# A macaron block with a state-space layer on one Trainium2 core: turning the down projection's result by 32x32 blocks and a round trip through HBM

## The chip, the cores and the metric

The kernel runs on one core of a Trainium2 chip. The metric is device time in microseconds (us) of the whole program, which is one launch. The engines of the core are called PE (TensorE, matrix products), DVE (VectorE), ACT (ScalarE), POOL (GpSimd) and SP (SyncE, which in this kernel issues nearly all DMAs).

## The reference

The input `u` is two sequences of 1024 rows with 1024 columns, 2048 rows in all, in fp32. Three residual steps follow each other:

```python
x = x + 0.5 * ffn(layernorm(x))      # gate, up and down: 4-bit weights, INTER = 2752
x = x + s4(layernorm(x))             # a causal filter along each row, by a Toeplitz product
x = x + 0.5 * ffn(layernorm(x))      # the same weights again

def ffn(x):
    h = silu(x @ Wg) * (x @ Wu)      # 1024 -> 2752
    return h @ Wd                    # 2752 -> 1024
```

The weights are stored as packed 4-bit numbers with a scale and a zero point for each group of 128 input rows and each output column. The result is fp32.

## The kernel before, in words

The 2048 rows are four blocks `b` of TB = 512 rows. A feed-forward pass over one block is a job; the list `JOBS` holds eight, `(0,1) (1,1) (0,3) (1,3) (2,1) (3,1) (2,3) (3,3)`, the second number being 1 for the first feed-forward of the block and 3 for the second. A block's filter (`convolve`) and layernorms are done in the shadow of another block's job.

**A job** has two stages. `gate_up(j, b, hooks)` runs 64 steps. A step is one wave of two or three 128-column groups with one of eight 128-row groups of the weights. In a wave of three there are six accumulators in PSUM and twelve matrix products in a step: each accumulator takes a product with the high part (`xTh`, fp32) and one with the low part (`xTl`, fp16) of the turned input (L753). After a step each accumulator is multiplied in place by the ratio of two groups' scales, by `scaled`: on ACT (L723) or on DVE (L725). Then the next step adds to it. `down(j, b, hooks)` runs 44 steps, `a` = 0, 1 for the two halves of 512 output columns and `f` = 0 to 21 for the rows of Wd. A step has four accumulators, `c` = 0 to 3, each with two products (`hl` and `hh`, L825) and one scaling; `c` = 0 and 2 go to ACT, `c` = 1 and 3 to DVE. At the last `f` the scaled result is written to SBUF: `yT[a, c]`, a tile of 128 output columns by 512 rows of the block. So the result lies turned, columns on partitions, while `x` has rows on partitions.

**Bringing the result back.** `back(b, a, t)` handles 128 rows and 512 columns. PE turns four 128x128 pieces of `yT` into a PSUM bank (L847), and DVE adds the bank to `x[b][t]` (L849). A job has eight calls, 2 halves by 4 values of `t`.

**The order around it.** Work of other stages is put into dictionaries of hooks, `up` and `dn`, by step number. A hook is called when its step is written, ahead of the step's products. `at(hooks, s, f)` adds one. The instructions of an engine then run in the order in which the tile scheduler puts them; `in_order_of_writing(f, engines)` pins the instructions of `f` to their written place on the engines named. Back of half 0 is at `dn` steps 26, 30, 34, 38 (32, 35, 38, 41 in job 0), after `load_x` has brought the block's `x` again at step 21; back of half 1 is at `up` steps 0 to 3 of the next job, and after the last job's end for the last one. For blocks whose first feed-forward is over, the next job's `up` also holds `moments` and `deviations` (layernorm statistics, at steps 4 and 5), and from step 8 (42 in job 1) `norm`, `swap` and `conv`, four steps for each `t`. `normalize` (L256) and `turn_by_dma` prepare the next job's input, the latter with POOL operations and transposing DMAs on SP at `dn` steps.

**The weights' supply.** `next_weights` issues on SP the load of the bytes for four steps ahead (`b<-wq`, `bd<-wdq`) and writes the cast to fp32 on POOL for three steps ahead (L701).

**Buffers.** `ypool` has four tiles of 128x512 fp32; `convolve` takes two of them for each `t`. `xpool` has ten tiles of 128x1024, `hpool` 44 tiles of 128x512.

Of the kernel before, what the change touches and what calls it, by code (L numbers as in the profile page):

```python
# [24 lines left out]
P = 128  # L25
# [3 lines left out]
TB = 512  # L29
# [11 lines left out]
EIGHT = 8.0  # L41
LIFT = 2.0**20
NST = 64
EPS = 1e-5
LOG2E = 1.4426950408889634
LN2_HI = 0.693359375
# [9 lines left out]
def macaron_s4_kernel(  # L56
# [43 lines left out]
    qpool = ctx.enter_context(tc.tile_pool(name="q", bufs=4))  # L100
    gpool = ctx.enter_context(tc.tile_pool(name="g", bufs=3))
    hfpool = ctx.enter_context(tc.tile_pool(name="hf", bufs=3))
    ypool = ctx.enter_context(tc.tile_pool(name="y", bufs=4))
    ppool = ctx.enter_context(tc.tile_pool(name="ps", bufs=1, space=PSUM))
    dpool = ctx.enter_context(tc.tile_pool(name="dram", bufs=1, space=DRAM))

# [310 lines left out]
    def scales_down():  # L417
        ps = bank("ps_d")
        for i in range(2):
            row = t2(f"drow_{i}")  # L420
            nc.sync.dma_start(row[:GD], down_s[:, bass.ts(i, 512)])
            for k in range(4):
                nc.tensor.transpose(
                    ps[:, bass.ts(4 * i + k, GD)], row[:GD, bass.ts(k, P)], ident[:GD, :GD]
                )
        n = NC * GD
        flat = s_dn.rearrange("p c g -> p (c g)")
        nc.vector.tensor_copy(flat, ps[:, :n])
        inv = t2("inv_d")[:, :n]
        inverse(inv, flat, "d")  # L430
        inv = inv.rearrange("p (c g) -> p c g", c=NC)
        nc.vector.tensor_tensor(
            ratd[:, :, : GD - 1], s_dn[:, :, : GD - 1], inv[:, :, 1:], ALU.mult
        )
        nc.vector.tensor_scalar(
            ratd[:, :, GD - 1 :], s_dn[:, :, GD - 1 :], 0.5 / EIGHT, None, ALU.mult
        )
# [44 lines left out]
    def units(w):  # L482
# [2 lines left out]
        return got + [2 * WIDE] * (w == len(WAVES) - 1)  # L485

    width_of = lambda w: len(units(w)) * P
    w_q = [
        dpool.tile([HID, width_of(w)], I8, tag=f"wq{w}", name=f"wq{w}") for w in range(len(WAVES))
    ]  # L490
# [142 lines left out]
    def dequantize_down(a, rt, j):  # L633
        src = packed[a, rt][j % 2][:, j // 2, :]
        n = src.shape[0]
        q = qpool.tile([P, 512], I8, tag="q", name=f"qd_{a}_{rt}_{j}")[:n]
        nc.gpsimd.tensor_copy(q, src)
        rows = wd_q[a][8 * P * rt : 8 * P * rt + 8 * n]
        nc.sync.dma_start(rows.rearrange("(r j) n -> j r n", j=8)[j], q)
        if j == 7:  # L640
            packed.pop((a, rt))
# [75 lines left out]


    h = {}

    def scaled(on_act, dst, src, sc):
        if on_act:
            nc.scalar.activation(dst, src, AF.Copy, scale=sc)  # L723
        else:
            nc.vector.tensor_tensor(dst, src, sc.to_broadcast([P, TB]), ALU.mult)  # L725

    def gate_up(j, b, hooks):
        hi, lo = pieces[b]
        ps = {}
        for s, (wi, g) in enumerate(STEPS):  # L730
            w = next_weights()
            for hook in hooks.get(s, ()):
                hook()
            fs = WAVES[wi]
            n = len(fs)
            order = [(2 * f + i, i * n + u) for u, f in enumerate(fs) for i in range(2)]
            if wi == len(WAVES) - 1:
                order.append((2 * WIDE, 2 * n))


            early = len(order) // 2
            turns = [(k, pos, k == 1) for k in range(2) for pos in range(early)]
            turns += [(k, pos, k == 0) for k in (1, 0) for pos in range(early, len(order))]
            for k, pos, done in turns:
                unit, col = order[pos]
                if g == 0 and unit not in ps:
                    ps[unit] = acc(f"pg_{j}_{unit}")
                p = ps[unit]
                weights = w[:, bass.ts(col, P)]
                if k == 0:  # L750

                    weights = weights.bitcast(BF16).rearrange("p (n k) -> p k n", k=2)[:, 1, :]
                nc.tensor.matmul(  # L753
                    p,
                    weights,
                    (lo, hi)[k][:, g, :],
                    start=(g == 0 and not done),
                    stop=(g == GK - 1 and done),
                    skip_group_check=True,
                )  # L760
                if not done:
                    continue
                if g < GK - 1:
                    on_act = unit % 2 == 0
                    if pos == 1:
                        on_act = (j == 0 and g % 4 == 0) or (j == 1 and s < 32 and g % 2 == 0)
                    if unit == 2 * WIDE:
                        on_act = g % 2 == 0
                    scaled(on_act, p, p, rat[:, unit, g : g + 1])
                elif unit == 2 * WIDE:  # L770
                    gated_half(j, ps[unit])
                    give_back(ps.pop(unit))
                elif unit % 2:
                    gated(j, unit // 2, ps[unit - 1], ps[unit])
                    give_back(ps.pop(unit - 1), ps.pop(unit))
        pieces.pop(b)
# [37 lines left out]
    def down(j, b, hooks):  # L814

        steps = [(a, f) for a in range(NH) for f in range(NF)]
        for d, (a, f) in enumerate(steps):
# [3 lines left out]
            if f == 0:  # L821
                ps = [acc(f"po_{j}_{a}_{c}") for c in range(4)]
            for c in range(4):
                for k, part in enumerate(reversed(h[f])):
                    nc.tensor.matmul(  # L825
                        ps[c],
                        w[:, bass.ts(c, P)],
                        part,
                        start=(f == 0 and k == 0),
                        stop=(f == NF - 1),  # L830
                        skip_group_check=True,
                    )
                on_act = c % 2 == 0 or (j == 0 and c == 1 and f % 2 == 0)
                if f < GD - 1:
                    scaled(on_act, ps[c], ps[c], ratd[:, 4 * a + c, f : f + 1])
                elif f == NF - 1:
                    y = ypool.tile([P, TB], F32, tag="y", name=f"y_{j}_{a}_{c}")
                    scaled(on_act, y, ps[c], ratd[:, 4 * a + c, GD - 1 :])
                    yT[a, c] = y
                    give_back(ps[c])  # L840
        h.clear()

    def back(b, a, t):

        ps = bank(f"pb_{b}_{a}_{t}")
        for c in range(4):
            nc.tensor.transpose(ps[:, bass.ts(c, P)], yT[a, c][:, bass.ts(t, P)], ident)  # L847
        part = x[b][t][:, bass.ts(a, 512)]
        nc.vector.tensor_tensor(part, part, ps, ALU.add)  # L849

    near = const.tile([P, 4, P], F32, tag="near", name="near")
    after = const.tile([P, 4, P], F32, tag="after", name="after")
# [279 lines left out]
    def convolve(b, t, s, name):  # L1137
# [1 line left out]

        sums = ypool.tile([P, TB], F32, tag="y", name=f"sums_{name}")
        sums = sums.rearrange("p (c t) -> p c t", c=4)
        quad = ypool.tile([P, TB], F32, tag="y", name=f"quad_{name}")
        quad = quad[:, : 2 * P].rearrange("p (c t) -> p c t", c=2)
        nc.gpsimd.tensor_tensor(sums[:, 0:3], s[:, 0:6:2, :], s[:, 1:6:2, :], ALU.add)
        nc.gpsimd.tensor_tensor(quad, s[:, 0:2, :], s[:, 2:4, :], ALU.add)
        nc.gpsimd.tensor_tensor(sums[:, 3], sums[:, 0], sums[:, 1], ALU.add)
# [266 lines left out]

    x_dram = [dpool.tile([P, HID], F32, tag=f"xs{t}", name=f"xs{t}") for t in range(TOK // P)]
    saved = lambda b: x_dram[b * NT : (b + 1) * NT]
    JOBS = [(0, 1), (1, 1), (0, 3), (1, 3), (2, 1), (3, 1), (2, 3), (3, 3)]

    def fast():  # L1420
        def store_half(t, a, queue):
# [4 lines left out]
        for j, (b, k) in enumerate(JOBS):  # L1426
# [4 lines left out]
            def at(hooks, s, f):  # L1431
                hooks.setdefault(s, []).append(f)

            if prev:
                pb, pk = prev
                for t in range(NT):
                    at(up, t, lambda t=t: back(pb, 1, t))
                if pk == 1:
                    late = 34 if j == 1 else 0
                    at(up, 4, lambda: moments(pb, 2))  # L1440
                    at(up, 5, lambda: deviations(pb, 2))
                    s4x, s4n = {}, {}

                    def norm(t):
# [23 lines left out]
                    at(up, late + 28, save)  # L1468
                else:

                    def store():
                        for t, dst in enumerate(rows_of(out, pb)):
                            nc.sync.dma_start(dst, x[pb][t])
                        x.pop(pb)

                    at(up, 4, store)
            if j == 0:
                rows = {3: srow_next}
                for first_use, s, k0, k1 in ((5, 0, 3, 9), (14, 6, 9, 15), (30, 11, 15, WIDE)):
# [18 lines left out]
            if after:  # L1498
# [22 lines left out]
                for t in range(NT):  # L1521
                    for half in range(2):
                        d, where = ((22 + 4 * t + 2 * half, dn), (3 * t + half, dn))[min(j, 1)]
                        if j > 1:
                            d, where = 31 + 2 * t + half, up
                        piece = lambda t=t, half=half: normalize(ab, t, half)
                        piece = lambda piece=piece: in_order_of_writing(piece, ET.DVE)
                        at(where, d, piece)
# [10 lines left out]
            for d in (1, 2) if j else ():  # L1539
                piece = lambda j=j: next(half_split[j], None)  # L1540
                at(dn, d, lambda piece=piece: in_order_of_writing(piece, ET.Pool))
            o, gap = (27, 3) if j == 0 else (21, 4)
            at(dn, o, lambda: load_x(b, rows_of(u, b) if k == 1 else saved(b)))
            for t in range(NT):
                at(dn, o + 5 + gap * t, lambda t=t: back(b, 0, t))
                if not after:
                    first_half = lambda t=t: store_half(t, 0, nc.sync)
                    at(dn, o + 6 + gap * t, first_half)
            gate_up(j, b, up)
            down(j, b, dn)  # L1550
        for t in range(NT):
            back(b, 1, t)
            store_half(t, 1, (nc.sync, nc.scalar)[t % 2])

    STARTING = ET.Activation, ET.DVE, ET.SP
# [200 lines left out]
```

## Time and profile before

| | |
|---|---|
| time, median of 3 runs | 2096.85 us (2094.32 to 2098.55) |
| span of the profiled execution | 2095.8 us; its own time outside the profile is not given |
| mean granted TensorE clock | 0.998 |
| PE busy | 2054.6 us, 98% of the span |
| DVE busy | 1671.5 us, 80% |
| ACT busy | 1398.9 us, 67% |
| POOL busy | 1291.6 us, 62% |
| DMA moved | 151.03 MB, 24.7% of 16 engines' span on the main queue |

Busy time is the time in which an engine has at least one instruction at work. PE's matrix products overlap each other in the records, so a product of 435 ns costs less than that on the path: twelve in a row take about 2.7 us. The chain of waits is the better view for PE, since it splits the path without overlap.

### The profile page before, as it was taken

What the parts mean: (1) busy time and instruction counts of PE and PEld (TensorE: products, weight loads), DVE (VectorE), ACT (ScalarE), POOL (GpSimd) and SP (SyncE); (2) the same over time, 40 slices, a digit from 0 to 9 for tenths busy, and PEclk for the clock granted to TensorE, in tenths of its full rate; (3) what the DMA queues carried; (4) which work ended last, traced back from release to release, by engine and by line L of the source; (5) the groups of instructions that cost most, each with busy time, mean ns of one, the idle gap of its engine ahead of it and who ended that gap; (6) DMA issues with size and microseconds to landing.
All of it is one profiled execution on the core that took longest, in us unless ns stands there. A gap on an engine that the chain in (4) does not pass through costs nothing.

```text
span 2095.8 us, 30242 instructions
## 1 busy us (share of the span) xinstructions
PE 2054.6 (98%) x9556; PEld 1410.6 (67%) x9556; DVE 1671.5 (80%) x2749; ACT 1398.9 (67%) x2185; POOL 1291.6 (62%) x1688
## 2 busy tenths in 40 slices
PE   6999999999999999999999999999999999999998
PEld 4555775677776578655876568675686766866576
DVE  8888887778888877797778878878788787777776
ACT  6777777746655776667667776547765467667775
POOL 5867758657754577555955568455684546845542
PEclk9999999999999999999999999999999999999999
DMA  4324321113411126211441124111151111531111
GB/s 144 119 85 146 111 66 54 36 56 74 110 39 55 32 53 170 72 31 36 122 137 37 31 51 126 44 51 32 46 130 37 51 39 35 133 128 36 33 35 60
DMA packets 239719, 151.03 MB, mean 72 GB/s; under 512 B 98747, under 2 KB 226596, under 8 KB 239550
## 3 DMA queue, kind: packets, MB, share of 16 engines
q1 hardware_dynamic: 238246, 146.60, 24.7%
q8 instruction: 78, 1.28, 0.3%
q10 hardware_dynamic: 1016, 1.82, 0.2%
q14 instruction: 91, 0.75, 0.1%
q0 software_dynamic: 288, 0.59, 0.1%
HBM read 104.45 MB, written 25.50 MB: 62 GB/s over the span
## 4 chain that ended last, share of the span: by engine, by line
PE 92%; DVE 4%; DMA 1%; ACT 1%; issue 1%; POOL 0%; SPq 0%; ACTq 0%; DVEq 0%; POOLq 0%
PE pg L753 56%; PE po L825 29%; PE pc L1151 3%; PE pb L847 1%; PE pb L1151 1%; DVE pg L725 1%; PE st L230 1%; DMA b<-wq 1%; ACT g L780 0%; DVE po L725 0%; DVE x L256 0%; DMA x<-in_L_attn_u_dram 0%; POOL q L608 0%; DVE hf L783 0%; PE pt L230 0%
## 5 line engine op out<-in xcount | busy, mean ns | idle before, releaser
L723 ACT ACTIVATE pg<-pg,rat 128x512 f32<-128x512 f32 x1240 | 787.5, 661 | 418.1 <-PE pg L753 415.9
L725 DVE TENSOR_TENSOR pg<-pg,rat 128x512 f32<-128x512 f32 x1168 | 776.6, 693 | 159.3 <-PE pg L753 153.4
L753 PE MATMUL pg<-xTh,w_up 128*128 128x512 f32 x2752 | 840.5, 435 | 1.1 <-DVE pg L725 0.7
L753 PE MATMUL pg<-xTl,w_up 128*128 128x512 f16 x2752 | 716.7, 382 | 11.6 <-DVE pg L725 5.6
L701 POOL CAST w_up<-b 128x768 fp32r<-128x768 int8 (+2 forms) x490 | 378.0, 777 | 504.6 <-PE pg L753 405.7
L753 PEld LDWEIGHTS pg<-xTh,w_up 128*128 128x128 f32 x2752 | 518.3, 189 | 175.9 <-DVE pg L725 12.2
L723 ACT ACTIVATE po<-po,ratd 128x512 f32<-128x512 f32 x660 | 431.8, 661 | 164.7 <-PE po L825 164.1
L825 PE MATMUL po<-hl,w_down 128*128 128x512 f32 x1344 | 530.5, 397 | 3.7 <-DVE po L725 3.6
L825 PE MATMUL po<-hh,w_down 128*128 128x512 f32 x1344 | 521.2, 390 | 0.0
L725 DVE TENSOR_TENSOR po<-po,ratd 128x512 f32<-128x512 f32 x620 | 430.4, 698 | 113.3 <-PE po L825 109.1
L753 PEld LDWEIGHTS <-w_up 128*128 128x128 bf16 x2752 | 228.4, 99 | 330.3 <-issue 151.0
L701 POOL CAST w_down<-bd 128x512 fp32r<-128x512 int8 x352 | 218.4, 624 | 158.5 <-PE po L825 90.4
L825 PEld LDWEIGHTS po<-hl,w_down 128*128 128x128 f32 x1344 | 251.2, 188 | 73.3 <-DVE po L725 12.2
L825 PEld LDWEIGHTS po<-hh,w_down 128*128 128x128 f32 x1344 | 252.6, 188 | 49.0
L787 POOL TENSOR_TENSOR hl<-hf,hh 128x512 fp32r<-128x512 f32 x168 | 217.9, 1297 | 8.0
L783 DVE SCALAR_TENSOR_TENSOR hf<-pg,rat,g 128x512 f32<-128x512 f32 x168 | 123.2, 749 | 49.3 <-ACT g L780 40.4
L780 ACT ACTIVATE g<-pg,rat 128x512 f32<-128x512 f32 x168 | 111.0, 687 | 48.5 <-PE pg L753 32.8
L785 POOL CAST hh<-hf 128x512 fp32r<-128x512 f32 x168 | 106.1, 632 | 55.0 <-PE pg L753 31.0
L282 POOL TENSOR_TENSOR lo<-x,hi 128x512 f16<-128x512 f32 x48 | 62.2, 1296 | 0.0
L187 DVE BATCH_NORM_STATS2 stats<-x 128x6 f32<-128x512 f32 x88 | 60.0, 682 | 0.5
L280 POOL TENSOR_TENSOR mid<-hi,top 128x512 bf16<-128x512 f32 x48 | 56.4, 1174 | 0.0
L296 POOL TENSOR_TENSOR xTh<-turned 128x512 fp32r<-128x512 bf16 x48 | 55.9, 1165 | 0.0
(216 smaller groups left out, 1104.2 us busy)
## 6 DMA issues: line engine op xcount, KB each, us to landing
b<-wq SPq DMA_DIRECT2D x319, 96.0 KB
bd<-wdq SPq DMA_DIRECT2D x336, 64.0 KB
x<-in_L_attn_u_dram SPq DMA_DIRECT2D x30, 512.0 KB
b<-wq SPq DMA_DIRECT2D x128, 64.0 KB
xs<-x SPq DMA_DIRECT2D x16, 512.0 KB
x<-xs SPq DMA_DIRECT2D x16, 512.0 KB
out_dram<-x SPq DMA_DIRECT2D x12, 512.0 KB
b<-wq SPq DMA_DIRECT2D x64, 80.0 KB
```

The source lines that it names most:

```text
L187: nc.vector.bn_stats(stats[:, t, i, :], x[b][t][:, bass.ts(i, 512)])
L282: nc.gpsimd.tensor_tensor(lo[:, own], n[:, own], hi[:, own].bitcast(F32), ALU.subtract)
L701: nc.gpsimd.tensor_copy(t, b)
L723: nc.scalar.activation(dst, src, AF.Copy, scale=sc)
L725: nc.vector.tensor_tensor(dst, src, sc.to_broadcast([P, TB]), ALU.mult)
L753: nc.tensor.matmul(p, weights, (lo, hi)[k][:, g, :], start=(g == 0 and not done), stop=(g == GK - 1 and done), skip_group_check=True,)
L780: nc.scalar.activation(g, pg, AF.Silu, scale=rat[:, 2 * f, GK - 1 :])
L783: nc.vector.scalar_tensor_tensor(hf, pu, last, g, ALU.mult, ALU.mult)
L785: nc.gpsimd.tensor_copy(hi, hf)
L787: nc.gpsimd.tensor_tensor(lo, hf, hi.bitcast(F32), ALU.subtract)
L825: nc.tensor.matmul(ps[c], w[:, bass.ts(c, P)], part, start=(f == 0 and k == 0), stop=(f == NF - 1), skip_group_check=True,)
L1151: nc.tensor.matmul(dst, lhsT, rhs, start=start, stop=stop, skip_group_check=True)
```

## The change

Half results are no longer turned by PE, but for the last half of the last job.

- `yT[a]` is one tile of 128 x 2048 fp32 (`ypool` with one buffer). The weights' columns of Wd are stored in a permuted order (`by_block`, `by_chunk`), by `dequantize_down` on POOL and by `scales_down` on DVE, so that the four 32-row bands of the partitions and the four `c` hold columns that come out in sequence.
- The last scaling writes each `c` in runs of 32 (`block_of`). `turn_block` then turns eight 32x32 blocks in place with one DVE instruction on 128x256 elements; there are eight for each half.
- `rows_out` stores a band of 32 partitions to `y_dram[a]`, 256 KB in runs of 512 bytes, four DMAs on SP for each half. `rows_in` loads 128 rows by 512 columns, 256 KB, four for each half, into tiles of `hpool`.
- `back` is now a DVE addition on 128x256 with both inputs in SBUF, eight for each half. The last half of the last job keeps the products (`back_by_products`).
- `rows_home` puts these at steps: half 0 at `dn` 22 to 25.5 (turn), 27 and 28 (out), 31 and 32 (in), 34.5 to 41.5 (add); half 1 at `up` 0 to 3.5, 5 and 6, 8 and 9, 10 to 13.5 of the next job. Job 0's half 0 and job 1's half 1 have spacings of their own. Hooks may now stand at half steps: `gate_up` and `down` call those of `s + 0.5` in the middle of a step.
- Moved with it: in jobs 2, 5 and 6 the first `moments` of the filter goes from step 4 to pinned pieces at steps 14 to 19, and what follows it 14 steps later; in job 1 it goes to steps 30 to 38. In these jobs `normalize` for a second feed-forward goes from `up` step 31 to 45. The stores of finished blocks go from one hook at step 4 to four at steps 13 to 16. In jobs 2, 5 and 6 at steps 10 to 19, every second step's accumulator at place 1 is scaled on ACT.
- `convolve` takes its two temporaries from the one `y` tile.

The diff, cut to its core:

```diff
-    ypool = ctx.enter_context(tc.tile_pool(name="y", bufs=4))
+    ypool = ctx.enter_context(tc.tile_pool(name="y", bufs=1))
...
+            nc.vector.tensor_copy(by_chunk(turn[:GD]), by_block(row[:GD]))
...
+    by_block = lambda a: a.rearrange("p (a c i) -> p a c i", a=NQ, i=Q)
+    by_chunk = lambda a: a.rearrange("p (c a i) -> p a c i", a=NQ, i=Q)
...
-        nc.gpsimd.tensor_copy(q, src)
+        nc.gpsimd.tensor_copy(by_chunk(q), by_block(src))
...
+                        on_act = on_act or (j in (2, 5, 6) and 10 <= s < 20 and g % 2 == 0)
...
-                    y = ypool.tile([P, TB], F32, tag="y", name=f"y_{j}_{a}_{c}")
-                    scaled(on_act, y, ps[c], ratd[:, 4 * a + c, GD - 1 :])
-                    yT[a, c] = y
+                    if c == 0:
+                        yT[a] = ypool.tile([P, 4 * TB], F32, tag="y", name=f"y_{j}_{a}")
+                    if by_products(j, a):
+                        y = yT[a][:, bass.ts(c, TB)]
+                        scaled(on_act, y, ps[c], ratd[:, 4 * a + c, GD - 1 :])
+                    else:
+                        y, p = block_of(yT[a], c), ps[c].rearrange("p (t i) -> p t i", i=Q)
+                        scaled(on_act, y, p, ratd[:, 4 * a + c, GD - 1 :])
...
+    def block_of(y, c):
+        return y.rearrange("p (t c i) -> p t c i", c=4, i=Q)[:, :, c]
+    def turn_block(a, i):
+        c, half = divmod(i, 2)
+        part = block_of(yT[a], c)[:, bass.ts(half, TB // Q // 2)]
+        nc.vector.transpose(part, part)
+    def rows_out(a, q):
+        src = yT[a][bass.ts(q, Q)].rearrange("p (t n) -> p t n", n=P)
+        dst = y_dram[a].rearrange("(t i) (a n) -> a i t n", i=Q, n=P)[q]
+        nc.sync.dma_start(dst, src)
+    def rows_in(b, a, t):
+        rows_back[a, t] = r = t2(f"yr_{b}_{a}_{t}")
+        nc.sync.dma_start(r, y_dram[a][bass.ts(t, P)])
-    def back(b, a, t):
-        ps = bank(f"pb_{b}_{a}_{t}")
-        for c in range(4):
-            nc.tensor.transpose(ps[:, bass.ts(c, P)], yT[a, c][:, bass.ts(t, P)], ident)
-        part = x[b][t][:, bass.ts(a, 512)]
-        nc.vector.tensor_tensor(part, part, ps, ALU.add)
+    def back(b, a, i):
+        t, half = divmod(i, 2)
+        own = bass.ts(half, 256)
+        part = x[b][t][:, bass.ts(a, 512)][:, own]
+        nc.vector.tensor_tensor(part, part, rows_back[a, t][:, own], ALU.add)
...
-                for t in range(NT):
-                    at(up, t, lambda t=t: back(pb, 1, t))
+                turned_at = [i / 2 for i in range(8)]
+                added_at = [10 + (i if j == 1 else i / 2) for i in range(8)]
+                rows_home(at, up, pb, 1, turned_at, (5, 5, 6, 6), (8, 8, 9, 9), added_at)
...
-            o, gap = (27, 3) if j == 0 else (21, 4)
+            turned_at = [22.5 + i if j == 0 else 22 + i / 2 for i in range(8)]
+            added_at = [37.5 + (3 * i // 2) / 2 if j == 0 else 34.5 + i for i in range(8)]
+            out_at, in_at = (((31, 31, 32, 32), (35, 35, 36, 36)), ((27, 27, 28, 28), (31, 31, 32, 32)))[min(j, 1)]
+            rows_home(at, dn, b, 0, turned_at, out_at, in_at, added_at)
```

## The prediction

> **What bounds the kernel now.** I read the page first: busy time, then the chain of waits.
>
> ```profile
> PE 2054.6 (98%) x9556; PEld 1410.6 (67%) x9556; DVE 1671.5 (80%) x2749; ACT 1398.9 (67%) x2185; POOL 1291.6 (62%) x1688
> ...
> PE 92%; DVE 4%; DMA 1%; ACT 1%; issue 1%; POOL 0%; SPq 0%; ACTq 0%; DVEq 0%; POOLq 0%
> ```
>
> PE is the busiest engine and 92% of the path. What one `back` costs there is in the chain in order of time, here around half 0 of job 2:
>
> ```profile
> 799.88 0.91 PE po L825 x4
> 800.79 0.44 PE pb L847 x4
> 801.23 7.31 PE po L825 x32
> 808.54 0.44 PE pb L847 x4
> 808.98 3.20 PE po L825 x14
> ```
>
> Products run back to back, 7.31 us for 32 or 0.228 us each, and the four turns of a call stand in the row with 0.44 us. Time taken off PE is time off the end, as long as nobody else makes PE wait. How often, and what DVE does with it, is in the groups by line:
>
> ```profile
> L849 DVE TENSOR_TENSOR x<-x,pb 128x512 f32<-128x512 f32 x64 | 43.2, 679 | 6.3 <-PE pb L847 6.3
> L847 PE MATMUL pb<-ident,y 128*128 128x128 f32 x256 | 41.9, 276 | 0.2 <-ACT y L723 0.2
> ...
> L1186 DVE TENSOR_TENSOR x<-x,pb 128x256 f32<-128x256 f32 x16 | 6.7, 420 | 1.6
> ```
>
> 256 turns are 64 calls. What is added is paid on DVE, so its spare time comes next, in its timeline at the same place:
>
> ```profile
> 798.11 0.70 DVE L725 TENSOR_TENSOR po<-po,ratd 128x512 f32<-128x512 f32 x1 [0.21 <-PE po L825]
> 799.01 0.70 DVE L725 TENSOR_TENSOR po<-po,ratd 128x512 f32<-128x512 f32 x1 [0.21 <-PE po L825]
> ...
> 800.83 0.70 DVE L725 TENSOR_TENSOR po<-po,ratd 128x512 f32<-128x512 f32 x1 [0.21 <-PE po L825]
> 801.44 0.68 DVE L849 TENSOR_TENSOR x<-x,pb 128x512 f32<-128x512 f32 x1
> ```
>
> Queued instructions start before the one ahead has ended: 800.83 to 801.44 is 0.61 us for one of 0.70. An instruction thus takes its duration less 0.09 us of DVE. A down step is 1.81 us (8 x 0.227) and holds two scalings, 1.22 us; **0.59 us are spare**. A gate-up step of 12 products is 2.71 us and holds three, 1.83; 0.88 us are spare. There is slack too: a down accumulator is used again 6 products (1.36 us) after it is done, the scaling takes 0.70 after a start delay of 0.21, so DVE may be 0.45 us late; in gate-up 8 or more products lie between, which gives 0.9 us. Last, the DMA engines, by stretches (PE, PEld, DVE, ACT, POOL busy, clock, DMA share, GB/s), with 4 KB rows coming in and with the 512-byte rows of the down weights alone:
>
> ```profile
> 792.00:794.00 2.00, 2.00 (x10) 1.67 (x9) 0.88 (x2) 1.11 (x2) 1.86 (x4) 1.00 0.96 371
> 808.00:810.00 2.00, 2.00 (x13) 1.65 (x12) 1.70 (x4) 1.18 (x2) 1.85 (x3) 1.00 0.11 33
> ```
>
> [...] `normalize`, SBUF to SBUF, has a smallest of 529 ns, a median of 540 and a largest of 1480, while L849 and L1186, with one input in PSUM, keep within a few per cent.
>
> ```profile
> L256 DVE TENSOR_SCALAR x<-x,mv,r x56: 529/540/1480, 248.4 to 1714.4; 128x512 f32<-128x512 f32 x56
> ```
>
> **The change part by part.**
>
> 1. *PE's turns.* The last half of the last job keeps 4 calls, so 60 go: 60 x 0.44 = **26.4 us** off the path. With them goes a shadow: after each call of half 0 the 0.68 us addition exceeds the spare 0.59, and the next 32 products take 7.31 instead of 7.25 us; 32 calls x 0.06 = 1.9 us. Sum -28.3. Bounds -26 and -30, the latter if the first turns of a job, which wait for ACT's last scaling, cost more than 0.44.
>
> 2. *`turn_block`*, 15 halves x 8 = 120 DVE instructions on 128x256 fp32, not seen before. Low price 0.42 us, that of L1186 with the same elements[...]. High price 0.70, if [...] 256 behave as 512. I take 0.42. Two stand in each of four steps. Down: 2 x 0.33 = 0.66 against 0.59 spare, 0.07 x 4 = 0.3 us late, under the slack of 0.45: **nothing**. Gate-up: 0.66 against 0.88: nothing. Without that cover, at 0.70: down 2 x 0.61 - 0.59 = 0.63 a step, 2.5 in four less 0.45 is 2.1 us x 7 jobs = 14; gate-up 1.22 - 0.88 = 0.34, 1.4 less 0.9 is 0.5 x 7 = 3. High end +17.
>
> 3. *The additions*, 120 of 128x256 for 60 of 128x512, and both inputs now in SBUF. Alone about 0.42 us (as L1186; the source is another). [...] `normalize` averages 713 ns (39.9 us for 56), 0.18 over its smallest, and I take the same. Down, one a step: 0.42 - 0.09 + 0.18 = 0.51 against 0.59 fits on average, but waits come in bunches, and POOL is busy there for 1.85 us of 2 (the stretch at 808): I take 0.4 us for each of 8 halves, **+3**. Gate-up, two a step for four steps: 1.02 against 0.88, 0.6 late in all, under 0.9: nothing. [...] Bounds 0 and +10.
>
> 4. *The trip.* SP gets four `rows_out` and four `rows_in` for each half, 120 DMAs. One half is 1 MB each way. From the stretch above, 33 GB/s at a share of 0.11 is 300 GB/s for 512-byte rows: 3.5 us out, and some 3 us in. 15 x 6.5 = 98 us of the engines' time, 5% on top of 25. Time allowed: in `dn` out at 27 and 28, in at 31 and 32, first addition at 34.5: 3.5 steps, 6.3 us, from the first load's issue. In `up` in at 8, added at 10: 5.4 us. Behind a waiting `rows_out` or `rows_in` stand SP's weight loads (four steps ahead, so 7 us in down and 11 in gate-up hide it) and, for half 0, the transposing DMAs of `turn_by_dma`; behind a waiting addition stand DVE's scalings, then PE. **Nothing**, as all has steps of time; below nothing isn't possible. High end in the rivals.
>
> 5. *What moves.* The pinned statistics (8 x 0.60 + 4 x 0.12 = 5.3 us over six steps of 0.88, five scalings of these and the steps before on ACT, which is busy 19.09 us in ten steps of 27.1) fit. The filter keeps its work and its own waits. `yT` with one buffer is written 17 or more steps after its last reader is issued. The permuted casts and the strided last scaling keep their element counts. The four stores now at 13 to 16 and the later loads on SP wait for nothing that is late. +1 (bounds -2 and +4). The tail keeps its turns; a store of half 0 now stands at the last step, +0.5 (0 to +1.5).
>
> Against the profiled execution: 2095.8 - 28.3 + 0 + 3 + 0 + 1.5 = 2072.0. The median of the runs shown, 2096.85, is 1.05 over that span, so I write 2073. About 0.2%, 4 us, is what a measurement of this kernel can tell from no change.
>
> **Rivals.** *A: the block turn is slow* (0.70). For it: fp32, strided, in place, unseen. [...] 2073 + 17 = 2090. *B: rows come late, slower.* An addition whose rows haven't landed stops DVE's queue and then PE, 15 times. If the first load takes 10 us to land instead of 5: 4.6 - 0.9 = 3.7 in `up` and 3.7 - 0.45 = 3.2 in `dn`, 7 x 3.7 + 8 x 3.2 = 52, 2125. It decides from a lateness of 24/15 + 0.7 = 2.3 us, a landing 8 us after issue. For it: DMA share 0.96 when `load_x` runs, transposing DMAs near `dn` 28 and 34. Against: the same stretches show 2 MB of `x` passed in 6 us, and between the steps of the trip a share of 0.11 to 0.83. *C: [...]*, POOL's long instructions (1.3 us at L787, 1.2 at L280) being hit nearly each time: 0.5 more for each addition, 8 halves x 0.9 and 7 x 0.9 give +10 over my +3: 2083. *D: the time doesn't leave*: DVE becomes the bound of both stages and PE waits where it turned. For it 80% busy; against it the 0.59 and 0.88 us. About 2094.
>
> **How the numbers follow.** My forecast 0.63 (2068 to 2080), A 0.14, C 0.10, D 0.05, B 0.08. The range takes the forecast, C and most of A: 2066 to 2091. Faster by over 0.2%: forecast, A, C and a little of D, 0.88; same: most of D, 0.04; slower: B, 0.08.
>
> **What would show it.** L847 with 16 instead of 256; the block turns at about 0.42 us; 7.25 us for 32 products around `dn` 22 to 42; DVE's idle before the additions without a DMA as its cause; additions with a spread like `normalize`'s. Wrong it is if the chain shows DVE scalings (L725's successor) with several per cent, or additions released by `yr<-yz` loads.

## The result, and the profile after

| | before | after |
|---|---|---|
| time, median of 12 runs each | 2097.35 us (2094.32 to 2100.47) | 2098.70 us (2094.89 to 2103.68) |
| span of the profiled execution | 2095.8 us | 2097.1 us |
| mean granted TensorE clock | 0.998 | 0.996 |
| DMA moved | 151.03 MB | 182.47 MB |

The ratio is 1.0007, with a 95% interval of 0.9998 to 1.0015: no difference that can be told. The prediction had 2073 us, a range of 2066 to 2091, and 0.88 for faster. It was wrong, by 26 us.

The page of the kernel after, its busy times and its chain of waits by engine:

```profile
PE 2044.3 (97%) x9316; PEld 1378.3 (66%) x9316; DVE 1722.2 (82%) x2916; ACT 1405.3 (67%) x2200; POOL 1301.5 (62%) x1688
...
PE 86%; DVE 7%; DMA 2%; POOL 2%; issue 1%; ACT 1%; SPq 0%; ACTq 0%; POOLq 0%; DVEq 0%
```

PE has 240 instructions less, so the turns are gone. Yet the chain, which ran through PE for 92% of the span, now does so for 86%; DVE has gone from 4 to 7%, DMA and POOL by one or two. PE is given less to do and waits instead. The groups by line of the kernel after have the new instructions (L875 is `turn_block`, L893 the addition in `back`, L899 the turns that remain):

```profile
L893 DVE TENSOR_TENSOR x<-x,yr 128x256 f32<-128x256 f32 x120 | 73.1, 615 | 3.0 <-DMA yr<-yz 3.0
L875 DVE STREAM_TRANSPOSE y<-y 128x256 f32<-128x256 f32 x120 | 51.6, 431 | 0.0
L899 PE MATMUL pb<-ident,y 128*128 128x128 f32 x16 | 2.0, 278 | 0.1
```

All three are near the prices forecast: 0.43 us for a block turn (0.42), 0.615 for an addition (0.42 + 0.18), 16 turns instead of 256. DVE sat idle for the rows once, for 3.0 us. So the mean prices of the pieces don't explain the loss, and it had to be looked for by stage.

**Where the time is, by stage.** For each stage I take the time from its first product to the next stage's first in the trace and subtract 0.2265 us for each product (688 in gate-up; 344 in down, as the last step of each half has four products, not eight). What is left, the excess, is all else that PE does or waits for there, and what a lower clock costs. A half brought back by PE has 16 turns in the excess, 4 x 0.44 = 1.76 us; the third row takes them off.

| excess, us | job 0 gate-up | job 1 gate-up | jobs 2, 5, 6 gate-up | jobs 3, 4, 7 gate-up | eight downs |
|---|---|---|---|---|---|
| before | 20.8 | 37.2 | 94.4 | 6.7 | 44.3 |
| turns to be taken off | 0 | 1.8 | 5.3 | 5.3 | 14.1 |
| before less turns | 20.8 | 35.4 | 89.1 | 1.4 | 30.2 |
| after | 21.5 | 45.0 | 95.2 | -0.3 | 43.3 |
| lost again | 0.7 | 9.6 | 6.1 | -1.7 | 13.1 |

The losses sum to 27.8 us against turns of 26.5, and the difference is that of the two spans. Only in the gate-ups of jobs 3, 4 and 7, where no layernorm or filter was moved, did the forecast come true: after the change PE runs there with nothing between the products. Three places took it back: down (13.1), job 1's gate-up (9.6) and the gate-ups of jobs 2, 5 and 6 (6.1).

**The clock's part.** For a few stretches of 3.4 or 6.8 us the profile gives PE half the clock, and products that else start 0.22 us apart start 0.43 us apart. The longest within the stages of the kernel after, by `--windows` (busy PE, PEld, DVE, ACT, POOL, then the clock, DMA share, GB/s):

```profile
418.80:425.60 6.80, 6.28 (x19) 3.94 (x18) 5.59 (x9) 2.52 (x4) 3.50 (x5) 0.50 0.14 39
```

At these starts such a stretch costs about half its length, an estimate. Before, 1.7 us of job 1's excess are of this kind; after, 3.4 of job 1's and 1.7 of job 0's. So of the 9.6 us lost in job 1, 7.9 are left for waits. Whether waits of PE bring the lower clock about was not tested: `e5_moves_alone`, below, has the same waits at the same place and keeps the full clock there.

**Down, the block turns.** DVE's timeline of the kernel after, at two turns a step in job 2:

```profile
806.22 0.67 DVE L733 TENSOR_TENSOR po<-po,ratd 128x512 f32<-128x512 f32 x1
806.79 0.42 DVE L875 STREAM_TRANSPOSE y<-y 128x256 f32<-128x256 f32 x1
807.14 0.67 DVE L733 TENSOR_TENSOR po<-po,ratd 128x512 f32<-128x512 f32 x1
807.72 0.42 DVE L875 STREAM_TRANSPOSE y<-y 128x256 f32<-128x256 f32 x1
808.19 0.70 DVE L733 TENSOR_TENSOR po<-po,ratd 128x512 f32<-128x512 f32 x1
```

Steps 24, 25 and 27 of the down stages of jobs 1 to 7 are each longer than eight products by 0.16 to 0.20 us, 0.54 in all. A scaling usually starts 0.43 us after its accumulator's second product does; in job 2 those of steps 22 to 24 start 0.20 to 0.25 us later than that, which the prediction's slack of 0.45 covers. What PE does at the end of step 24 shows more:

```profile
806.93 0.39 PE L840 MATMUL po<-hh,w_down 128*128 128x512 f32 x1
807.23 0.70 PE L840 MATMUL po<-hl,w_down 128*128 128x512 f32 x2
807.76 0.62 PE L840 MATMUL po<-hh,w_down 128*128 128x512 f32 x2
```

and ACT beside it:

```profile
806.42 0.66 ACT L729 ACTIVATE po<-po,ratd 128x512 f32<-128x512 f32 x1 [0.25 <-PE po L840]
```

In nearly all steps `hl` and `hh` take turns. Here two `hl` follow each other: the first product of step 25 stands ahead of the last accumulator's two of step 24. It needs ACT's scaling, which is at its usual time and ends at 807.08; PE comes two products too early and waits for it (the trace has its wait for ACT's semaphore over at 807.12), and its load of weights starts at 807.20, 0.50 us after the one before it; loads usually follow each other by 0.23. The products at 807.23 and 807.54 start 0.30 and 0.31 us after those before them instead of 0.23. Step 25 shows the same wait for ACT, and step 27 one for a scaling of DVE that is not late. The scheduler puts PE's instructions in this order when the program is built; with no block turns (e3, below) or one a step (e11, e8) it is regular in these steps and nothing is lost. Why the scheduler changed it, and what a pinned order would give, no run here shows.

Job 0 is another case. Its block turns stand at one a step, where DVE also unpacks weights and runs `normalize`; steps 24 to 27 have an excess of 3.5 us, and 1.0 in e3.

**Down, the additions.** DVE's timeline a little later in the same stage, and POOL's beside it:

```profile
837.58 0.97 DVE L893 TENSOR_TENSOR x<-x,yr 128x256 f32<-128x256 f32 x1
838.47 1.28 DVE L733 TENSOR_TENSOR po<-po,ratd 128x512 f32<-128x512 f32 x2
839.67 0.97 DVE L893 TENSOR_TENSOR x<-x,yr 128x256 f32<-128x256 f32 x1
```

```profile
837.11 1.16 POOL L298 TENSOR_TENSOR xTh<-turned 128x512 fp32r<-128x512 bf16 x1
838.21 1.02 POOL L706 CAST w_up<-b 128x768 fp32r<-128x768 int8 x1
```

The mean of 615 ns hid two kinds: 0.41 to 0.43 us for half of them, and mostly 0.74 to 0.97 here, where POOL is never idle. POOL's L298 of 837.11 ends at 838.27, and the addition that came in 0.47 us after it began ends only at 838.55. With two scalings, 1.22 us, a step has 0.59 us to give. In job 2 steps 36, 38, 41 and 42 lose 0.17 to 0.29 us each.

At steps 36 to 39 POOL is busy because its work comes late. Its timeline a little before, at step 32:

```profile
821.79 0.61 POOL L706 CAST w_down<-bd 128x512 fp32r<-128x512 int8 x1 [2.55 <-DMA bd<-wdq]
```

The stores and loads of the trip stand in SP's queue ahead of the loads of weights, so POOL's cast waits for its bytes, and what POOL does for the next job's input comes out later, beside the additions. The list of waits (us in total, times, longest) has for these bytes, before, after, and in e2 below, which leaves out the trip:

```profile
POOL w_down L701 <- DMA bd<-wdq: 3.5, 1, 3.5
POOL w_down L706 <- DMA bd<-wdq: 22.1, 11, 3.8
POOL w_down L706 <- DMA bd<-wdq: 0.5, 1, 0.5
```

**Job 1's gate-up and jobs 2, 5, 6: the moved chains.** `guess` and `deviations`, which turn variances into reciprocal roots, are 13 instructions of 128x4, four elements for each partition. Before, the 13 took 2.3 to 3.4 us of DVE in sum in jobs 1 to 6; after, 7.3 for the filter in job 1 and 4.3 to 4.8 for the third layernorm in jobs 2, 5 and 6. (The filter's own chain in those three jobs fits at its new steps, with 3.2 us.) The chain of waits in order of time, after, in job 1 (L214 to L216 are these instructions, "e" and "r" their tiles):

```profile
415.06 1.21 DVE e L214
416.27 0.61 DVE pg L733
416.88 0.07 DVE e L215
416.95 0.02 issue
416.98 1.20 DVE r L216
418.17 0.61 DVE pg L733
```

and POOL's timeline of the kernel after at the same time:

```profile
414.97 1.28 POOL L799 TENSOR_TENSOR hl<-hf,hh 128x512 fp32r<-128x512 f32 x1
416.19 0.61 POOL L797 CAST hh<-hf 128x512 fp32r<-128x512 f32 x1
416.88 1.27 POOL L799 TENSOR_TENSOR hl<-hf,hh 128x512 fp32r<-128x512 f32 x1
```

An instruction with a median of 0.16 us is on the chain for 1.2 us: 415.06 + 1.21 = 416.27, and POOL's instruction ends at 414.97 + 1.28 = 416.25. The next: 418.18 against 418.15. Each of the 17 long ones in jobs 1 to 6 (0.70 to 1.28 us) ends 0.01 to 0.03 us after a POOL instruction that was already at work when it began. The additions of this kernel show the same kind of wait: of the 54 that took over 0.5 us, 53 end 0.27 to 0.29 us after the POOL instruction that was at work when they began; of the 63 that took under 0.45 us, 32 began beside a POOL instruction, and it had at most 0.16 us left. Each such wait also holds DVE's queue, with the scalings of PE's accumulators in it: the scaling of 416.27 starts as the long instruction ends.

Job 1 has one more loss: DVE's single wait for rows. The chain in order of time, after, in job 1, step 11 of gate-up:

```profile
320.32 2.66 DMA yr<-yz
...
323.01 0.95 DVE x L893
323.96 0.62 DVE pg L733
```

### The profile page after: what moved, and what is told of

Read it like the earlier page. It is cut to its first block, busy times and chain, and to the rows that moved or that the text cites. A ratio compares the mean times of both kernels' runs of the same rounds, so it can differ in the third digit from the quotient of the medians.

```text
span 2097.1 us, 30092 instructions
## 1 busy us (share of the span) xinstructions
PE 2044.3 (97%) x9316; PEld 1378.3 (66%) x9316; DVE 1722.2 (82%) x2916; ACT 1405.3 (67%) x2200; POOL 1301.5 (62%) x1688
## 2 busy tenths in 40 slices
DMA packets 280039, 182.47 MB, mean 87 GB/s; under 512 B 100667, under 2 KB 259236, under 8 KB 279870
## 4 chain that ended last, share of the span: by engine, by line
PE 86%; DVE 7%; DMA 2%; POOL 2%; issue 1%; ACT 1%; SPq 0%; ACTq 0%; POOLq 0%; DVEq 0%
PE pg L764 52%; PE po L840 28%; PE pc L1197 3%; DVE pg L733 2%; PE pb L1197 1%; DMA bd<-wdq 1%; DVE po L733 1%; PE st L232 1%; DVE x L893 1%; DMA b<-wq 1%; POOL q L613 0%; POOL hl L799 0%; DVE x L258 0%; DVE ve L199 0%; DMA x<-in_L_attn_u_dram 0%
## 5 line engine op out<-in xcount | busy, mean ns | idle before, releaser
L733 DVE TENSOR_TENSOR pg<-pg,rat 128x512 f32<-128x512 f32 x1153 | 765.4, 693 | 140.8 <-PE pg L764 130.8
L764 PE MATMUL pg<-xTh,w_up 128*128 128x512 f32 x2752 | 856.3, 439 | 7.3 <-DVE pg L733 4.4
L733 DVE TENSOR_TENSOR po<-po,ratd 128x512 f32<-128x512 f32 x620 | 425.9, 694 | 91.0 <-PE po L840 88.2
L840 PEld LDWEIGHTS po<-hl,w_down 128*128 128x128 f32 x1344 | 250.2, 188 | 94.4 <-DVE po L733 29.3
L799 POOL TENSOR_TENSOR hl<-hf,hh 128x512 fp32r<-128x512 f32 x168 | 219.2, 1305 | 7.2
L797 POOL CAST hh<-hf 128x512 fp32r<-128x512 f32 x168 | 108.7, 647 | 53.9 <-DVE hf L795 28.3
L893 DVE TENSOR_TENSOR x<-x,yr 128x256 f32<-128x256 f32 x120 | 73.1, 615 | 3.0 <-DMA yr<-yz 3.0
L298 POOL TENSOR_TENSOR xTh<-turned 128x512 fp32r<-128x512 bf16 x48 | 56.5, 1177 | 0.0
```

The source lines that it names most:

```text
L733: nc.vector.tensor_tensor(dst, src, sc.to_broadcast(list(dst.shape)), ALU.mult)
L764: nc.tensor.matmul(p, weights, (lo, hi)[k][:, g, :], start=(g == 0 and not done), stop=(g == GK - 1 and done), skip_group_check=True,)
L797: nc.gpsimd.tensor_copy(hi, hf)
L799: nc.gpsimd.tensor_tensor(lo, hf, hi.bitcast(F32), ALU.subtract)
L840: nc.tensor.matmul(ps[c], w[:, bass.ts(c, P)], part, start=(f == 0 and k == 0), stop=(f == NF - 1), skip_group_check=True,)
L893: nc.vector.tensor_tensor(part, part, rows_back[a, t][:, own], ALU.add)
```

## The experiments

The theory was by now: PE's turns were worth their full length, and (a) down has too little DVE time for turns and additions, (b) the moved layernorms cost far more than the 1 us given to them. Rivals: the turns were never worth 26 us; the trip through HBM costs the time. The kernel before, run beside them, had medians of 2096.59 to 2097.84. The diffs are cut to their core.

**e4_one_turn: were PE's turns worth their length?** The kernel before with one turn of four; the addition reads that block four times.

```diff
-        for c in range(4):
-            nc.tensor.transpose(ps[:, bass.ts(c, P)], yT[a, c][:, bass.ts(t, P)], ident)
+        nc.tensor.transpose(ps[:, :P], yT[a, t][:, bass.ts(t, P)], ident)
```

> The kernel before, with one of the four PE turns of each call of back; the addition on VectorE keeps its 128x512 and reads the turned block four times (three of four column blocks of Down's result are left out). Theory (PE's time is worth its full length; the gain was made and lost again elsewhere): 192 turns less at 0.44/4 us each, 21 us, so about 2076. Rival (the turns stood in time that PE had anyway): no change, 2097.

Measured 2077.33 us, ratio 0.9905 [0.9889, 0.9922]. The chain in order of time of this kernel, around half 0 of job 2, shows 0.11 where 0.44 stood:

```profile
799.61 0.11 PE pb L846
799.72 7.30 PE po L825 x32
807.02 0.11 PE pb L846
```

192 turns at 0.11 are 21 us, and 20 came. Step 1 of the prediction holds.

**e1_no_add, e2_no_trip, e3_no_turn: one part of the change taken away each.** The edits delete the line that places `back`; place neither `rows_out` nor `rows_in` and add `yT[a]` in place of the rows; delete the line that places `turn_block`.

> The changed kernel without the additions of half results to x (Down's result is left out but for the last half; block turns, rows out and rows in stay). Theory [...]: some 1.1 us in each of 8 down stages and 3 us in job 1 come back, about 2086. Rival (the trip through HBM delays the weights and so PE): the DMAs are all still there, 2097.

> The changed kernel without the rows out and in: the additions read the turned tile in SBUF instead of the rows loaded back, same shapes and same steps (the columns and rows added are then the wrong ones). Theory (the loss is on VectorE's queue): only the wait of job 1's first addition for its rows goes, 2 to 3 us, about 2095. Rival (the trip's 30 MB are what eats the gain): the 26 us come back, about 2073.

> The changed kernel without the block turns on VectorE (the rows stored are unturned, so what is added is in the wrong places). Theory: the turns cost 0.5 us in each of seven down stages and some 2 us in job 0's, nothing in gate-up: 5 to 6 us less, about 2092. Rival (VectorE has the room that the prediction gave it): no change, 2098.

| | time, us | ratio to before | eight downs, excess | job 1 gate-up, of it clock | jobs 2, 5, 6 gate-up |
|---|---|---|---|---|---|
| after | 2098.70 | 1.0007 [0.9998, 1.0015] | 43.3 | 45.0, 3.4 | 95.2 |
| e1_no_add | 2089.20 | 0.9965 [0.9951, 0.9979] | 35.9 | 41.9, 1.7 | 95.2 |
| e2_no_trip | 2095.46 | 0.9991 [0.9982, 1.0000] | 40.7 | 45.5, 5.1 | 95.6 |
| e3_no_turn | 2087.03 | 0.9960 [0.9946, 0.9974] | 32.4 | 43.6, 0.0 | 95.4 |

The additions are worth 9.5 us by the medians: 7.4 in down, and 1.4 in job 1 beside the clock, where the wait for the rows goes with them. The block turns are worth 11.7 by the medians, twice what I expected, and 10.9 by the downs. Of these, 2.8 are in job 0 and 3.8 in steps 24 to 27 of the other seven jobs; most of the rest is in the steps of the additions: without the turns the stores leave at step 22, and POOL's waits for `bd<-wdq` sum to 6.9 us instead of 22.1. The trip is worth about 3, 2.6 of it in down, so it is not the main cause; but what it costs there it costs by way of POOL. In e2 and in e3, where the loads of weights are not held back at that place, the additions at steps 37.5 to 39.5 of jobs 1 to 6 take 0.41 to 0.42 us, in the kernel after mostly 0.72 to 0.88. So the parts overlap. None of the three touches jobs 2, 5 and 6. In e3 job 1's gate-up is 2.0 us longer beside the clock, for which I have no cause.

**e5_moves_alone: the moved layernorms without the change.** The kernel before, with the moves of statistics, filter, `normalize` and stores, and the extra scalings on ACT, and nothing else. Cut to its core:

```diff
-                    late = 34 if j == 1 else 0
-                    at(up, 4, lambda: moments(pb, 2))
-                    at(up, 5, lambda: deviations(pb, 2))
+                    late = 34 if j == 1 else 14
...
+                    in_pieces(at, steps, lambda: moments_by_tile(pb, 2, halves=True))
+                    at(up, late + 7, pinned(lambda: deviations(pb, 2), ET.DVE))
...
-                            d, where = 31 + 2 * t + half, up
+                            d, where = (45 if ak == 3 else 31) + 2 * t + half, up
```

> The kernel before with what the change moves and nothing else: the statistics, the filter, normalize and the stores of finished blocks at their new steps, and the scalings given to ScalarE; PE turns the results as before. Theory (the moved layernorm chains now meet GpSimd's long instructions): 2.3 us in each gate-up of jobs 2, 5 and 6 and some 4 us in job 1's, 11 in all, about 2108. Rival (moving is free, as the prediction had it): 2097.

Measured 2111.95 us, ratio 1.0075 [1.0058, 1.0091]: the moves alone cost 14 us, where the prediction had 1. The chain in order of time of this kernel, in job 1, has the same waits, with no block turn and no row from HBM in it:

```profile
414.29 1.21 DVE e L212
...
416.21 1.20 DVE r L214
```

By stage, 7.0 us of it are in the gate-ups of jobs 2, 5 and 6 and 3.9 in job 1's, which is 5.6 beside the clock (before had a halved stretch there, e5 none). Another 3.3 stand in job 0's gate-up, which none of the moves touches: the clock was halved there for 6.8 us, 3.4 lost, as in the profile of e4, which is 2.7 us longer there. So the moves cost some 11 to 13 us.

**e6_chains_moved: the chains at other steps.** The kernel after; job 1's statistics at 18 to 25 and its chain at 28, and in jobs 2, 5 and 6 the second chain at 44 and 45, with `normalize` from 47.

```diff
-                    first = 30 if j == 1 else 14
+                    first = 18 if j == 1 else 14
...
-                    at(up, late + 7, pinned(lambda: deviations(pb, 2), ET.DVE))
+                    at(up, 28 if j == 1 else late + 7, pinned(lambda: deviations(pb, 2), ET.DVE))
...
+                        at(up, 44, pinned(lambda: next(third[0], None), ET.DVE))
+                        at(up, 45, pinned(lambda: deviations(pb, 3, LIFT), ET.DVE))
...
-(45 if ak == 3 else 31) + 2 * t + half
+(47 if ak == 3 else 31) + 2 * t + half
```

> The changed kernel with the layernorm chains at other steps: in job 1 the statistics at steps 18 to 25 and the chain at 28, in jobs 2, 5 and 6 the first guess of the third layernorm at step 44, its chain at 45 and normalize two steps later, past GpSimd's work at a wave's end. Theory: some 5 us in job 1 and 1.5 to 2 in each of three jobs come back, about 2088. Rival (the loss of those jobs is the filter's or the trip's): 2098.

Measured 2089.75 us, ratio 0.9966 [0.9953, 0.9978]. DVE's timeline of this kernel in job 5, and POOL's:

```profile
1458.41 0.15 DVE L214 TENSOR_TENSOR e<-r 128x4 f32<-128x4 f32 x1
1458.59 0.16 DVE L215 TENSOR_TENSOR e<-e,ve 128x4 f32<-128x4 f32 x1
1458.69 0.70 DVE L733 TENSOR_TENSOR pg<-pg,rat 128x512 f32<-128x512 f32 x1
1459.30 0.15 DVE L216 SCALAR_TENSOR_TENSOR r<-e,r 128x4 f32<-128x4 f32 x1
```

```profile
1457.83 0.62 POOL L706 CAST w_up<-b 128x512 fp32r<-128x512 int8 x1 [1.06 <-PE pg L764]
1459.64 0.62 POOL L706 CAST w_up<-b 128x512 fp32r<-128x512 int8 x1 [1.20 <-PE pg L764]
```

The same instructions at 0.15 us: POOL has nothing here but a cast every 1.8 us. The 13 instructions, in sum, in four kernels:

| us of DVE for one chain | before | after | e5_moves_alone | e6_chains_moved |
|---|---|---|---|---|
| job 1, filter | 2.7 | 7.3 | 7.3 | 3.6 |
| job 2, third layernorm | 2.6 | 4.8 | 4.8 | 2.9 |
| job 5 | 2.6 | 4.3 | 4.3 | 2.1 |
| job 6 | 2.6 | 4.3 | 4.3 | 2.1 |

The excess of the gate-ups of jobs 2, 5 and 6 falls from 95.2 to 89.0, all that they had lost (before less turns: 89.1), and job 1's from 45.0 to 41.2, 1.7 of which is clock.

**e9_add_psum: is it the second input in SBUF that makes the additions of down long?** The kernel after, with half 0's additions reading a PSUM bank.

```diff
+        if a == 0:
+            if i == 0:
+                rows_back["ps"] = ps = acc(f"pa_{b}_{t}")
+                nc.tensor.transpose(ps[:, :P], yT[a][:, :P], ident)
...
+            wide = ps[:, :P].unsqueeze(1).to_broadcast([P, 2, P])
...
         nc.vector.tensor_tensor(part, part, rows_back[a, t][:, own], ALU.add)
```

> The kernel after, but half 0's additions of every job (8 each, in the second half of down) take their second input from a PSUM bank instead of from the rows in SBUF; the bank is filled by one PE turn of 128x128 per half (8 turns, 0.9 us in all) and read twice over by each addition, so the sums are not the reference's. The rows still go out and come home. Theory [...]: these additions fall from 0.75 to 0.97 us to about 0.42, a down stage's excess from 2.6 to about 1.4 us, the total is 2098 - 8 x 1.2 + 0.9 = 2089. Rival (the place in the step and DVE's queue count[...]): they still last over 0.6 us, total 2097.

Measured 2091.72 us, ratio 0.9976 [0.9967, 0.9986]. The group by line, and DVE's timeline of this kernel at the same steps of job 2:

```profile
L899 DVE TENSOR_TENSOR x<-x,pa 128x256 f32<-128x256 f32 x64 | 26.2, 410 | 0.0
```

```profile
835.35 0.41 DVE L899 TENSOR_TENSOR x<-x,pa 128x256 f32<-128x256 f32 x1
835.67 0.69 DVE L733 TENSOR_TENSOR po<-po,ratd 128x512 f32<-128x512 f32 x1
836.55 0.70 DVE L733 TENSOR_TENSOR po<-po,ratd 128x512 f32<-128x512 f32 x1 [0.18 <-PE po L840]
837.16 0.41 DVE L899 TENSOR_TENSOR x<-x,pa 128x256 f32<-128x256 f32 x1
```

All 64 take 0.41 us, at the same places, with DVE now waiting for PE (0.18) and not the reverse; a down stage's excess in jobs 2 to 6 is 1.4 to 1.5 us instead of 1.9 to 3.0. As many elements and as many additions, but no long one: it is where the second input lies.

**e7_add_later, e11_turn_spread, e8_all, e10_job1_later: other places.** e7 puts half 0's additions of jobs 1 to 6 at steps 4 to 9 of the next gate-up; e11 puts the block turns of half 0 in those jobs at one a step, out at 30 and 31, in at 33 and 34, and the additions at 36.5 to 43.5; e8 is e6 and e7 with one turn a step, out at 31 and 32, in at 35 and 36; e10 is e8 with job 1's additions three steps later. The lines of e7 and of e8:

```diff
+                added_at = [4 + (3 * i // 2) / 2 for i in range(8)]
...
-turned_at = [22.5 + i if j == 0 else 22 + i / 2 for i in range(8)]
+turned_at = [22.5 + i if j == 0 else 22 + i if after else 22 + i / 2 for i in range(8)]
```

> The changed kernel with the additions of half 0 of jobs 1 to 6 in the next job's gate-up (steps 4 to 9) instead of this job's down. Theory (the additions [...] do not fit the spare time of a down step, but fit a gate-up step's): down's excess falls to that without additions, 1.3 us in each of six, 8 us less, about 2090. Rival (they only move their wait to gate-up): 2098.

> The kernel after, with half 0's block turns of jobs 1 to 6 at one a down step (22 to 29) instead of two, out at 30 and 31, in at 33 and 34, additions at 36.5 to 43.5. Nothing is left out. Theory (two block turns in a step exceed DVE's spare 0.59 us and cost 0.17 to 0.19 us of PE in three or four steps): 6 x 0.6 = 3.6 us less, 2094. Rival (the cost of the turns is the DVE time itself, wherever it stands, or the later additions lose what the turns save): 2098.

> The two before together, and the block turns of half 0 in jobs 1 to 6 at one a step instead of two (rows out at 31 and 32, in at 35 and 36). Theory: the sum of the two, 18 us, and 0.7 us in each of six down stages, 4: about 2076, and faster than the kernel before by 1%. Rival (the trip through HBM or VectorE's total load bounds it): no better than the kernel before, 2097.

> e8 with one change: in job 1 the additions of half 1 of job 0 stand at gate-up steps 13 to 20 instead of 10 to 17, since the rows of the first one landed 3 us late there. Theory (the wait for the rows is a cost of its own): job 1's gate-up loses about 3 us of excess, 2080.5 - 3 = 2077. Rival (the stall comes back in a later place, as the statistics follow at step 18): 2080.

| | time, us | ratio to before |
|---|---|---|
| e7_add_later | 2093.95 | 0.9985 [0.9979, 0.9992] |
| e11_turn_spread | 2095.54 | 0.9996 [0.9987, 1.0004] |
| e8_all | 2080.46 | 0.9925 [0.9908, 0.9941] |
| e10_job1_later | 2080.64 | 0.9930 [0.9913, 0.9946] |

e7 brought 4.8 of the 8.7 us expected: the downs of jobs 2 to 6 fall to 1.3 or 1.4 us each, but job 1's gate-up keeps its stalls (43.7, none of it clock). e11 by itself is within the measurement; its trace shows steps 22 to 29 without a loss above 0.08 us, while additions at step 40 and after lose 0.9 to 1.0 us a stage. e8 is 0.75% faster than the kernel before and some 18 us faster than the kernel after by the medians, though 4 us short of what was expected. DVE's timeline of e8 at one turn a step:

```profile
807.54 0.70 DVE L733 TENSOR_TENSOR po<-po,ratd 128x512 f32<-128x512 f32 x1 [0.18 <-PE po L840]
808.15 0.43 DVE L875 STREAM_TRANSPOSE y<-y 128x256 f32<-128x256 f32 x1
808.50 0.67 DVE L733 TENSOR_TENSOR po<-po,ratd 128x512 f32<-128x512 f32 x1
809.35 0.70 DVE L733 TENSOR_TENSOR po<-po,ratd 128x512 f32<-128x512 f32 x1 [0.18 <-PE po L840]
```

Once in each step DVE waits for PE again, and the downs of jobs 2 to 6 have an excess of 0.7 us each, against 2.6 to 2.7 before, 1.76 of it turns. Job 0's down keeps 14.4, with its block turns where they were. Job 1's gate-up keeps 40.9, 5.5 us above the 35.4 that it could have. e10 tried to win that back and did not. Its chain in order of time in job 1 shows why:

```profile
330.35 1.53 DVE x L893
331.88 1.67 DVE s_cos L984 x2
333.55 1.78 DVE pg L733 x3
```

The wait for the rows is gone, but the addition stands at 1.53 us among the pieces of the filter's tables (`s_cos`), which `s4_tables` puts into DVE's queue at job 1's steps 1 to 42. DVE is full there, and a later place only moves the stall.

## Why the prediction was wrong

- **Step 1, PE's turns, -28.3: right.** 192 of 256 turns were worth 20 us (e4), and the gate-ups of jobs 3, 4 and 7 lost their turns and gained nothing else.
- **Step 5, "What moves", +1 (bounds -2 and +4): the term that failed most.** It measured +14 by itself (e5), some 11 to 13 of it beside the clock. "The pinned statistics ... fit" prices 8 `bn_stats` and 4 `bn_aggr` instructions and holds: steps 14 to 19 of jobs 2, 5 and 6 lose nothing. The 13 small instructions that follow have no price. "The filter keeps its work and its own waits" put them at nothing, and that is the step that failed: their work stayed and their waits did not. At the new steps POOL makes `hh` and `hl` (L797, L799), and some of the 13 wait for it: in job 1 three take 1.2 us and four about 0.6. The prediction had the spread of `normalize`, 529 to 1480 ns, and applied it to the new additions only, not to the moved instructions.
- **Step 3, the additions, +3 (0 to +10): the right kind of wait and mean, mis-sized.** The mean of 615 ns is the forecast 0.60. But the long ones come together, in the steps where POOL is never idle, at 0.74 to 0.97 us; the price was 0.51 against 0.59 spare, with waits on average. Without them 9.5 us go (e1), about 7 with no more than half 0's second input taken from PSUM (e9). "Gate-up nothing" fails in job 1, where the filter's tables fill DVE, which the prediction did not look at.
- **Step 2, `turn_block`, 0: right price and right lateness, and still a cost.** The turns took 0.43 us, and DVE was 0.25 us late, under the slack, as forecast. But each half in the other seven downs lost 0.54 us, because PE's own instructions stood in another order in those steps, of which the prediction has no word. And its sums are for seven jobs; job 0's turns, at one a step among other work of DVE, have no term and cost 2.8 us. In jobs 1 to 6 one turn a step costs nothing that the trace shows (e11, e8).
- **Step 4, the trip, nothing: about 3 us (e2).** The prediction named the path, SP's loads of weights behind a waiting store or load, and said that four steps of lead hide it. They hide it from PE; POOL waited for the bytes, and its late work met the additions. The DMA engines also moved 169 to 173 GB/s while a half went out (812 to 820 us, job 2), where 300 were priced. The rows themselves came late once, by 3.0 us, in job 1; rival B, lateness 15 times, did not happen.
- **Rivals.** A fell by 0.43 us. C had POOL's long instructions, but gave them 10 us more in the additions and nothing in the moved work. D, "the time doesn't leave", had 0.05 and the nearest figure, 2094, but for another reason: DVE is 82% busy and not the bound of both stages. That its figure came near is luck.

By stage, the sum of 2072 allowed 3 us for the 13.1 that the downs lost, and 1 for the 15.7 of the gate-ups of jobs 1, 2, 5 and 6. Of these 15.7, 1.7 are clock, 12.6 are there with the moves alone (e5), and 1.4 go with the additions of job 1 (e1). The parts overlap, since each shifts the steps of the others, so that they nearly sum up is not a proof that nothing else is in them.

## What to carry to other kernels

Work that leaves the busiest engine pays only if the engine that takes it has the time in the very steps where it is put: count each step's instructions with what else the queue holds there, not with a stage's mean. A moved instruction is to be priced at its new place like a new one, and a small one above all: here one of 0.16 us took up to 1.28, by what POOL was doing there. A queue that is held up need not stop the busiest engine to cost something: look whose work it moves, and onto what. And where only one engine's order is pinned, read the others' order anew after a change. With their second input in PSUM all 64 additions of e9 took 0.41 us, and in e6, where POOL had only a cast every 1.8 us, the small instructions took 0.15 to 0.16; moving the chains by a few steps, half 0's additions into the next gate-up and the turns apart brought 0.9925, with nothing taken out.

## What the hardware showed that I had not expected

- A DVE instruction of 128x4 elements, usually 0.16 us, took up to 1.28 us, and the 17 that took 0.70 or more in jobs 1 to 6 ended 0.01 to 0.03 us after the POOL instruction at work when they started. `tensor_scalar` on int32 with one SBUF input (L202, L203) did so too, at 1.20 to 1.28 us.
- An in-place block turn of 128x256 fp32, strided by runs of 32, took 403 to 439 ns, as long as an addition of as many elements from PSUM (410).
- No block turn waited for POOL: all 120 took 403 to 439 ns, though 86 of them ran beside a POOL instruction, while additions with both inputs in SBUF took up to 1.33 us.
- At half the granted clock products started 0.43 us apart instead of 0.22, in stretches of 3.4 and 6.8 us, and such stretches alone put 3.3 us between two profiles in a stage that the edit leaves as it was (job 0's gate-up, before and e5).
